# Two transformer layers on one core: denominators of the first element, the projection's order, and a matmul behind its filler

## The chip, the cores and the metric

The kernel runs on one core of one Trainium2 chip. A core has a matmul engine (TensorE, PE in the profile), VectorE (DVE), ScalarE (ACT), GpSimd (POOL) and a queue engine for transfers (SyncE, SP). The metric is the device time of one launch in microseconds, lower being better; a change is named by its ratio to the time before. All data is fp32.

## The reference

Sixteen elements of shape 256 channels x 32 x 32, that is 1024 positions, go through two layers:

```python
# layer 0, 4 heads of 64
qkv = (xs @ w_proj + b_proj).reshape(B, S, 4, 3 * 64)
attn = softmax(einsum('bihd,bjhd->bijh', q, k) * 64 ** -0.5, axis=2)
res = einsum('bijh,bjhd->bihd', attn, v).reshape(B, S, 256)
x = res @ w_out + b_out + xs
...
# layer 1, 8 heads of 32
x = x + attention(group_norm(x, gn1_w, gn1_b), qkv_w, proj_w, proj_b, phys_bias)
h = group_norm(x, gn2_w, gn2_b)
h = gelu(einsum('oc,bchw->bohw', mlp_w1, h) + mlp_b1)
x = x + einsum('oc,bchw->bohw', mlp_w2, h) + mlp_b2
```

A softmax is an exponential divided by its row's sum. The kernel works with unnormalised exponentials, sums them, and multiplies the result of the attention by the inverse of the sum, called the denominator below (`den`). There is no search for a maximum; the sums of all denominators and of their inverses go into two totals (`dsum`, `isum`) that are looked at once at the end, and a second, general pass runs if they were out of range.

## The kernel before

**Stages.** The elements run one after the other, and the work of neighbours overlaps. For each element b: the first attention (`attention_a`, layer 0), projection of its result (`o`), a group norm, the second attention (`attention_b`, layer 1), its projection (`j`), a second group norm, and the MLP in two halves (`hidden`, `outputs`), whose matmuls use a seven-product scheme for 2x2 blocks. The MLP of element b is used as filler for element b+1: its first half fills the time between the two attentions, and its second half, pieces `m`, goes into the steps of the second attention. The input projections of the next element (`qk_a`, `v_a`; a list `first` of 12 pieces for element 0, eight for query and key and four for value) fill what is left. A piece of these is two matmuls of 128x128x512 (query, key) or four of 128x128x256 (value). Element 0 has no MLP before it: between its two attentions stand the 12 pieces of `first`, and the later steps of its second attention have no filler. Elements 1 to 14, "middle elements", are alike; their keys and queries are made by seven products.

**An attention.** The positions are worked in two query halves t of 512, and the heads in two channel groups c: four items. For each item the loop goes over eight blocks of 128 keys. `scores` gives `s` in PSUM, ScalarE the exponential `e`, `weigh` the product with the values (`acc`), and VectorE adds the exponentials into `es`. A step of the second attention takes two key blocks. After an item, TensorE sums `es` over the partitions into `den`.

**Inverting.** `denominators` (L375) has ScalarE copy `den` out of PSUM (L376), a transfer spreads it over all partitions (L381), VectorE inverts the 128x16 that come out (L387), transfers bring the inverse to DRAM and back, spread as wide as the result (L391 or L398, L403), and later `then` multiplies (L510 or L707). It is a chain of steps counted by `later.after(n, fn)`: `fn` runs at the n-th tick from then, and a step of an attention has one tick. In the first attention one `den` serves both items of a query half (`normalise`, L479). In the second attention of middle elements each item's `es` is first folded to half by two transfers into `packed` (`fold`, L651), the second of which adds; three or four ticks later `normalise_folded` (L659) makes `den`.

**Order inside a step.** `run` (L1253) ticks, which issues what is due, and then runs the step's filler pieces; each engine works through its instructions in the order they come in, apart from a scheduler that moves some of them where nothing forbids it.

**The projection.** `out_proj` (L737) makes two output halves co from two input halves kc, with 128x32 column tiles inside an attention (`cols[0]` below 128). There both output halves lie in one PSUM tile, and its loop is output half first: co 0 from kc 0, co 0 from kc 1, co 1 from kc 0, co 1 from kc 1. Input half kc 1 is the item normalised last. In middle elements the result goes by ScalarE into a place in `packed` (`home`, slots 2 and 3) and is added a step later.

**Places.** PSUM has two banks b0 and b1 and three tiles of two banks (`wide`). Scores of the first key block of a step of the second attention use b0 and b1, and a `wide`; `acc` uses b0; `den` of the second attention uses b1. `packed` has four slots: item 0's folded sums in 0 and 1, item 1's in 2 and 3, item 2's again in 0 and 1. Products 6 and 7 of the MLP put their results into slots 2 and 3 (`number - 4`), once `normalise_folded` of item 1 has declared the place as free.

Of the kernel before, what the change touches and what calls it, by code (L numbers as in the profile page):

```python
# [14 lines left out]
P = 128  # L15
# [4 lines left out]
TB = 512  # L20
# [239 lines left out]
def first_pass(ctx, tc, x, out, k):  # L260
# [109 lines left out]
    def weights_tile(name):  # L370
        return work.tile([P, 4, TB], F32, tag="e", name=name, bufs=4)

    spread_out, spare = {}, {}

    def denominators(key, den, d, full, waits, then, parts=1):  # L375
        nc.scalar.copy(d, den)  # L376
# [34 lines left out]

    def attention_a(b, qT, kT, v, project):
        key, D, lag = f"a_{b}", D0, 2
        items = [(t, c) for t in range(NT) for c in range(CC)]
        units = [(i, kb) for i in range(len(items)) for kb in range(SB)]
        res = act.tile([P, CC, S], F32, tag="res", name=f"res_{key}")
        accs, held, sums, both, pair = {}, {}, {}, {}, []

        def scores(i, kb):
            t, c = items[i]
# [18 lines left out]
        def weigh(i, kb, e):  # L441
            t, c = items[i]
            if kb == 0:
                if i % 2:
                    acc = wide(f"acc_{key}_{i}", 2)
                    accs[i] = [acc[:, h, :] for h in range(2)]
                else:
                    accs[i] = [bank(f"acc_{key}_{i}_{h}", h) for h in range(2)]
            for h in range(2):
                for g in range(2):  # L450
                    nc.tensor.matmul(  # L451
                        accs[i][h][g * D : (g + 1) * D, :],
                        v[h * HALF : (h + 1) * HALF, kb, c * 2 + g],
                        e[h * HALF : (h + 1) * HALF, g, :],
                        start=(kb == 0),
                        stop=(kb == SB - 1),
                    )
            if kb == 0:
                held[i] = e
                return  # L460
            if kb == 1:
                if c == 0:
                    both[t] = work.tile([P, 2 * CC, TB], F32, tag="es", name=f"es_{key}_{t}", bufs=2)
                sums[i] = both[t][:, 2 * c : 2 * c + 2]
            spread_out["es"] = nc.vector.tensor_add(  # L465
                sums[i], held[i] if kb == 1 else sums[i], e
            )
            if kb == SB - 1:
                r = res[:, c, t * TB : (t + 1) * TB]
                one, two = accs.pop(i)  # L470
                nc.scalar.copy(r, one)
                nc.vector.tensor_add(r, r, two)  # L472
                if i == len(items) - 1:
                    kept.discard(2)
                if c == CC - 1:
                    later.after(2 if t < NT - 1 else 1, lambda: normalise(t))


        def normalise(t):  # L479
            half = TB // 2  # L480
# [63 lines left out]
    def attention_b(b, qT, kT, v, project):  # L544
# [106 lines left out]
        def fold(i, r):  # L651
            if i == 0:
                packs.append(act.tile([P, 4, TB], F32, tag="res", name=f"packed_{key}"))
            packed = packs[0][:, i % 2 * 2 : i % 2 * 2 + 2]
            nc.sync.dma_start(packed, sums[i][:HALF])
            nc.gpsimd.dma_start(packed, sums[i][HALF:], accum_op=ALU.add)
            later.after(3 if i == 1 else 4, lambda: normalise_folded(i, r, packed))

        def normalise_folded(i, r, packed):  # L659
            c = items[i][1]  # L660
            q = TB // G
            den = bank(f"den_{key}_{i}", 1)[:, :q]
            for m in range(2):
                for n in range(G):
                    nc.tensor.matmul(
                        den[n * D : (n + 1) * D, :], k["folded"][:, c, m],
                        packed[:, m, n * q : (n + 1) * q], start=m == 0, stop=m == 1,
                    )
            if i == 1:
                spare["home"] = packs[0]  # L670
            full = work.tile([P, TB], F32, tag="full", name=f"rd_{key}_{i}", bufs=2)
            denominators(
                f"{key}_{i}", den, full[:, :q], full, (1, 2 if i < 2 else 4),
                lambda full: scale(i, r, False, full), G,
            )

        def normalise(i, r, last):
            t, c = items[i]
            at_end = last and b == B - 1
            den = bank(f"den_{key}_{i}", 1)  # L680
            for g in range(G):
                nc.tensor.matmul(
                    den[g * D : (g + 1) * D, :],
                    k["eones"][:, c * G + g],
                    sums[i][:, g, :],
                    start=True,
                    stop=True,
                )
            full = work.tile([P, TB], F32, tag="full", name=f"rd_{key}_{i}", bufs=2)
            if at_end:  # L690

                nc.vector.reciprocal(full, den)
                scale(i, r, last, full)
                for tot, what in ((dsum, den), (isum, full)):
                    part = small.tile([P, 1], F32, tag="part", name="part")
                    nc.vector.tensor_reduce(part, what, AX.X, ALU.add)
                    nc.gpsimd.tensor_add(tot[:, :1], tot[:, :1], part)
# [39 lines left out]
    def out_proj(key, w, src, bias, xs, t, stats, then):  # L737
        todo = list(range(CC))

        def issue(cos=range(CC), apart=False):  # L740
            home = None if apart else spare.pop("home", None)
            apart = apart or cols[0] == P
            if not apart:
                both = wide(f"{key}_{t}")
            ps = {}

            def leave(co):
                y = xs[:, co, t * TB : (t + 1) * TB]
# [12 lines left out]
                todo.remove(co)  # L761

            def add_up(co, y, held):
                with tc.issue_after(spread_out["es"].ins):
                    nc.vector.tensor_add(y, y, held)
                    nc.vector.bn_stats(stats[:, co, t, :], y)

            for co in cos:
                ps[co] = bank(f"{key}_{t}_{co}", co) if apart else both[:, co, :]
                for kc in range(CC):  # L770
                    product(
                        ps[co],
                        w[:, kc, co * P : (co + 1) * P],
                        src(kc),
                        start=(kc == 0),
                        stop=(kc == CC - 1),
                    )
                if apart:
                    leave(co)
            if not apart:  # L780
                for co in cos:
                    leave(co)
            if not todo and then:
                then()
# [312 lines left out]
    def mlp(b, xb):  # L1097
# [93 lines left out]
        def reduce(number, right, outs, then, part=0, parts=1):  # L1191
# [14 lines left out]
            if len(outs) == 2 or "home" in spare:  # L1206
# [3 lines left out]
                if len(outs) == 2:  # L1210
                    m = lent[0][:, number % 4]
                else:
                    m = spare["home"][:, number - 4]
                if bias is not None:
                    nc.scalar.activation(m[:, at], ps, AF.Identity, bias=bias[:, co : co + 1])
                    bias = None
# [36 lines left out]
    def run(stage, fill=None):  # L1253
        for n, _ in enumerate(stage):
# [3 lines left out]
            later.tick()  # L1258
            if n <= last:
                run_pieces(pieces, False)  # L1260

    def run_pieces(pieces, tick=True):
        for piece in pieces:
# [79 lines left out]
    for b in range(B):  # L1343
        def load_next(b=b):
# [13 lines left out]
            attention_0(  # L1358
                b, tiles0, xs[b],
                lambda st, b=b, xn=xn, seven=seven, sums_1=sums_1: group_norm(  # L1360
                    f"g{b}", xs[b], st, k["g1w"], k["g1b"], "res", xn, 2 if b else 3,
                    (lambda y: sums_1.update(input_sums(f"b{b}", y))) if seven else None,
                ),
            )
# [43 lines left out]
        own = [lambda: early(v[1]), qk[n], v[2], qk[n + 1], v[3], *qk[n + 2 :]]  # L1408
        now, end = outputs, []
        if b == 0:  # L1410
            first = []
        if b == B - 1:

            now, end = outputs[:3], outputs[3:]
        if not first:

            fill = {m: [piece] for m, piece in enumerate(own[:5:2] + own[1::2] + own[6:])}
            fill.update({len(own) + 3 * m: [piece] for m, piece in enumerate(now)})
            now = []

        if first:
            o = [
                [lambda piece=piece, part=part: piece(part, 2) for part in range(2)]
                for piece in now
            ]
# [319 lines left out]
```

## Time and profile before

| | us |
|---|---|
| median of 3 runs | 3612.91 |
| lowest, highest | 3612.54, 3613.1 |
| the profiled execution's own time | 3610.05 |
| span of its instructions | 3608.0 |
| DVE add of exponentials in `attention_b`, 128x2048, 460 of them | 1.935 each |
| ACT exponential in `attention_b`, 1280 of them | 0.865 each |

The profile holds one execution. A line of its timeline has the start in us, the time from the first start to the last end of a group of like instructions, engine, source line, operation, output tile <- inputs, shape and count, and in brackets how long the engine stood idle before it and what ended that. PE is matmuls and PEld weight loads. A fp32 matmul leaves two records. Ends on PE are modelled, starts are measured. Times are counted from the start of the span.

### The profile page before, as it was taken

What the parts mean: (1) busy time and instruction counts of PE and PEld (TensorE: products, weight loads), DVE (VectorE), ACT (ScalarE), POOL (GpSimd) and SP (SyncE); (2) the same over time, 40 slices, a digit from 0 to 9 for tenths busy, and PEclk for the clock granted to TensorE, in tenths of its full rate; (3) what the DMA queues carried; (4) which work ended last, traced back from release to release, by engine and by line L of the source; (5) the groups of instructions that cost most, each with busy time, mean ns of one, the idle gap of its engine ahead of it and who ended that gap; (6) DMA issues with size and microseconds to landing.
All of it is one profiled execution on the core that took longest, in us unless ns stands there. A gap on an engine that the chain in (4) does not pass through costs nothing.

```text
span 3608.0 us, 81721 instructions
## 1 busy us (share of the span) xinstructions
PE 3584.1 (99%) x35573; PEld 1470.7 (41%) x35573; DVE 2780.1 (77%) x3181; ACT 2282.7 (63%) x3196; POOL 232.0 (6%) x317
## 2 busy tenths in 40 slices
PE   9999999999999999999999999999999999999999
PEld 4434344343443434434344443434434444343433
DVE  5686887868777687876878878688786977868787
ACT  4665757657575675756658566585765757657572
POOL 3000100001000010000000001000010100000000
PEclk9999999999999999999999999999999999999999
DMA  3010311213122131211312113121121212213100
GB/s 130 10 60 30 73 63 37 75 34 86 45 43 69 39 81 45 48 64 39 81 45 52 66 33 81 45 55 63 38 76 45 55 63 47 73 39 64 51 28 28
DMA packets 81572, 198.30 MB, mean 55 GB/s; under 512 B 37974, under 2 KB 38742, under 8 KB 75062
## 3 DMA queue, kind: packets, MB, share of 16 engines
q1 hardware_dynamic: 71828, 164.39, 14.6%
q0 software_dynamic: 7632, 28.21, 5.1%
q8 instruction: 281, 4.60, 0.5%
q14 instruction: 85, 0.70, 0.1%
q10 hardware_dynamic: 1746, 0.40, 0.1%
HBM read 125.85 MB, written 22.27 MB: 41 GB/s over the span
## 4 chain that ended last, share of the span: by engine, by line
PE 80%; DVE 10%; issue 5%; DMA 3%; SPq 2%; ACT 1%; DVEq 0%; POOL 0%
PE s_a L428 12%; PE acc_a L451 12%; PE m L1109 10%; PE s_b L571 8%; PE acc_b L625 7%; PE m L357 6%; DVE es_b L599 5%; PE qk_b L1015 3%; PE qk_a L1015 3%; PE v_b L357 3%; PE o L357 3%; PE j L357 3%; PE v_a L357 2%; DMA rd_b<-row_b 2%; PE qk7y_b L1015 1%
## 5 line engine op out<-in xcount | busy, mean ns | idle before, releaser
L584 ACT ACTIVATE e_b<-s_b 128x1024 f32<-128x1024 f32 (+1 forms) x1280 | 982.0, 865 | 136.9 <-PE s_b L571 136.3
L599 DVE TENSOR_TENSOR es_b<-es_b,e_b 128x2048 f32<-128x2048 f32 (+1 forms) x460 | 881.8, 1935 | 102.3 <-ACT e_b L584 85.9
L438 ACT ACTIVATE e_a<-s_a 128x1024 f32<-128x1024 f32 x512 | 520.7, 1024 | 361.0 <-PE s_a L428 359.0
L428 PE MATMUL s_a<-q,k 64*64 64x512 f32 x4096 | 544.2, 593 | 0.7 <-DVE res_a L472 0.7
L451 PE MATMUL acc_a<-e_a,v 64*64 64x512 f32 x4096 | 540.1, 589 | 0.0
L571 PE MATMUL s_b<-q,k 32*64 32x512 f32 x8192 | 527.3, 600 | 4.0 <-DVE res_b L643 2.0
L465 DVE TENSOR_TENSOR es_a<-es_a,e_a 128x1024 f32<-128x1024 f32 x384 | 470.4, 1225 | 70.7 <-ACT e_a L438 51.7
L625 PE MATMUL acc_b<-e_b,v 128*32 128x512 f32 x4096 | 492.1, 598 | 0.0
L357 PE MATMUL m<-g,w 128*32 128x256 f32 (+2 forms) x6464 | 416.6, 385 | 0.0
L357 PEld LDWEIGHTS m<-g,w 128*32 128x32 f32 (+1 forms) x6464 | 224.2, 111 | 203.8 <-issue 57.7
L451 PEld LDWEIGHTS acc_a<-e_a,v 64*64 64x64 f32 x4096 | 187.9, 133 | 251.5 <-issue 215.2
L571 PEld LDWEIGHTS s_b<-q,k 32*64 32x64 f32 x8192 | 175.7, 130 | 257.5 <-issue 132.7
L428 PEld LDWEIGHTS s_a<-q,k 64*64 64x64 f32 x4096 | 175.9, 133 | 247.5 <-issue 209.2
L625 PEld LDWEIGHTS acc_b<-e_b,v 128*32 128x32 f32 x4096 | 108.5, 109 | 351.5 <-ACT e_b L584 194.7
L1109 PE MATMUL m<-gn_h,w 128*128 128x512 f32 x512 | 242.2, 601 | 2.3 <-DVE x L1230 1.3
L599 DVE TENSOR_TENSOR es_b<-e_b,e_b 128x2048 f32<-128x2048 f32 (+1 forms) x72 | 147.0, 2052 | 124.5 <-ACT e_b L584 124.5
L1173 DVE TENSOR_TENSOR g<-g,g 128x512 f32<-128x512 f32 (+1 forms) x185 | 196.0, 1070 | 1.2 <-PE m L357 0.8
L1109 PE MATMUL m<-hs,w 128*128 128x512 f32 x384 | 178.1, 592 | 0.1
L1124 ACT ACTIVATE g<-g,m1b 128x512 f32<-128x512 f32 x128 | 92.1, 720 | 108.8 <-DVE g L1153 81.3
L1109 PEld LDWEIGHTS m<-gn_h,w 128*128 128x128 f32 x512 | 93.2, 190 | 117.7 <-issue 100.2
L1124 ACT ACTIVATE g<-m,m1b 128x512 f32<-128x512 f32 x128 | 80.9, 683 | 77.9 <-PE m L1109 77.9
L357 PE MATMUL v_a<-wp,x 128*32 128x256 f32 (+1 forms) x1856 | 121.5, 379 | 0.0
(217 smaller groups left out, 3537.8 us busy)
## 6 DMA issues: line engine op xcount, KB each, us to landing
w<-w_kept SPq DMA_DIRECT2D x30, 1792.0 KB
packed_b<-es_b SPq DMA_DIRECT2D x42, 512.0 KB
packed_b<-es_b POOLq DMA_DIRECT2D x42, 512.0 KB, 6.2
d_a<-row_a SPq DMA_DIRECT2D x64, 256.0 KB
rd_b<-row_b SPq DMA_DIRECT2D x252, 64.0 KB
out_dram<-x SPq DMA_DIRECT2D x63, 256.0 KB
x<-in_x_dram SPq DMA_DIRECT2D x30, 512.0 KB
qk<-qk_kept SPq DMA_DIRECT2D x14, 1024.0 KB
```

Of the source, the lines that this page charges most:

```text
L357: nc.tensor.matmul(o[sl], w[:, sl], r, **flags)
L428: nc.tensor.matmul(s[h : h + HALF, g, :], kT[g * D : (g + 1) * D, c, kb * P + h : kb * P + h + HALF], qT[g * D : (g + 1) * D, c, t * TB : ...
L438: nc.scalar.activation(e, s, AF.Exp, scale=float(D) ** -0.5)
L451: nc.tensor.matmul(accs[i][h][g * D : (g + 1) * D, :], v[h * HALF : (h + 1) * HALF, kb, c * 2 + g], e[h * HALF : (h + 1) * HALF, g, :], st ...
L465: spread_out["es"] = nc.vector.tensor_add(sums[i], held[i] if kb == 1 else sums[i], e)
L571: nc.tensor.matmul(outs[g][h : h + HALF, :], kT[g * D : (g + 1) * D, c, k0 : k0 + HALF], qT[g * D : (g + 1) * D, c, t * TB : (t + 1) * TB] ...
L584: spread_out["exp"] = nc.scalar.activation(to, s, AF.Exp, scale=float(D) ** -0.5)
L599: ins = nc.vector.tensor_add(d, (d if kb else es[0][:, g : g + step]), es[m][:, g : g + step])
L625: nc.tensor.matmul(acc[g * D : (g + 1) * D, :], v[:, kb + m, c * G + g], es[m][:, g, :], start=(m == 0), stop=(m == 1),)
L1015: nc.tensor.matmul(to, w, x[right], start=first, stop=True, skip_group_check=not first)
L1109: nc.tensor.matmul(ps, blocks[1][number - 1][:, i * P : (i + 1) * P], inputs[b][number], start=first, stop=True, skip_group_check=not first,)
L1173: (nc.vector.tensor_add if plus else nc.vector.tensor_sub)(d, d, more)
```

## The change

Element 0: in its first attention the second query half no longer takes the way through DMA. `normalise_item` makes a `den` for each of its two items. For the third item (first of the half) ScalarE copies `den` into SBUF and VectorE inverts the copy; for the fourth VectorE inverts from PSUM; then VectorE multiplies, and later reduces both for the totals (`add_to_range`, which also replaces the same lines in the last element). Five pieces of `first` stay between the attentions, and seven go into steps 8 to 14 of the second attention. The first group norm waits one tick in place of three.

All elements with a projection inside the attention: the loop is input half first, so both output halves from kc 0, then both from kc 1.

Middle elements: `normalise_folded` of item 1 is put on a list `trailing`, which `run` empties after the step's filler pieces. `packed` is declared as free for the filler when item 1 is folded, and product 6 writes slot 0 in place of 2.

```diff
@@ attention_a
+        def normalise_item(i):
+            t, c = items[i]
+            den = wide(f"den_{key}_{i}", next(m for m in order if m != 2))[:, 0, :]
+            for j in range(4):
+                nc.tensor.matmul(
+                    den[j * 32 : (j + 1) * 32, :], k["ones"], sums[i][:, j // 2, :],
+                    start=True, stop=True,
+                )
+            if not c:
+                homes.append(act.tile([P, CC, S], F32, tag="k1", name=f"d_{key}_{t}"))
+            full, held_den = homes[0][:, c, :TB], homes[0][:, c, TB:]
+            r = res[:, c, t * TB : (t + 1) * TB]
+            if c < CC - 1:
+                nc.scalar.copy(held_den, den)
+                den = held_den
+            tc.keep_in_program_order(nc.vector.reciprocal(full, den))
+            tc.keep_in_program_order(nc.vector.tensor_mul(r, r, full))
+            if c == CC - 1:
+                later.after(2, lambda: project(t, res)())
+            later.after(3, lambda: add_to_range(den, full))
...
-                if c == CC - 1:
+                if t == NT - 1 and not b:
+                    if c < CC - 1:
+                        later.after(2, lambda: normalise_item(i))
+                    else:
+                        normalise_item(i)
+                elif c == CC - 1:
                     later.after(2 if t < NT - 1 else 1, lambda: normalise(t))
@@ add_to_range
+    def add_to_range(den, inverse):
+        for tot, what in ((dsum, den), (isum, inverse)):
+            part = small.tile([P, 1], F32, tag="part", name="part")
+            nc.vector.tensor_reduce(part, what, AX.X, ALU.add)
+            nc.gpsimd.tensor_add(tot[:, :1], tot[:, :1], part)
@@ fold
-            later.after(3 if i == 1 else 4, lambda: normalise_folded(i, r, packed))
+            if i == 1:
+                spare["home"] = packs[0]
+                later.after(3, lambda: trailing.append(lambda: normalise_folded(i, r, packed)))
+            else:
+                later.after(4, lambda: normalise_folded(i, r, packed))
@@ out_proj
+            if apart:
+                for co in cos:
+                    for kc in range(CC):
+                        part(co, kc)
+                    leave(co)
+            else:
                 for kc in range(CC):
...
+                    for co in cos:
+                        part(co, kc)
                 for co in cos:
                     leave(co)
@@ reduce
-                    m = spare["home"][:, number - 4]
+                    m = spare["home"][:, number % 6 * 3]
@@ run
             if n <= last:
                 run_pieces(pieces, False)
+            while trailing:
+                trailing.pop(0)()
@@ the loop over elements
-                    f"g{b}", xs[b], st, k["g1w"], k["g1b"], "res", xn, 2 if b else 3,
+                    f"g{b}", xs[b], st, k["g1w"], k["g1b"], "res", xn, 2 if b else 1,
...
-            run_pieces(first if b == 0 else hidden)
+            run_pieces(first[:5] if b == 0 else hidden)
...
-            first = []
+            now, first = first[5:], []
...
-            fill.update({len(own) + 3 * m: [piece] for m, piece in enumerate(now)})
+            at = (len(own), 3) if b else (len(own) + 1, 1)
+            fill.update({at[0] + at[1] * m: [piece] for m, piece in enumerate(now)})
```

More of the change, by code (lines that the diff above doesn't have):

```diff
@@ L371, in weights_tile @@
         return work.tile([P, 4, TB], F32, tag="e", name=name, bufs=4)
-    spread_out, spare = {}, {}
+    spread_out, spare, trailing = {}, {}, []
     def denominators(key, den, d, full, waits, then, parts=1):
@@ L418, in attention_a @@
         res = act.tile([P, CC, S], F32, tag="res", name=f"res_{key}")
-        accs, held, sums, both, pair = {}, {}, {}, {}, []
+        accs, held, sums, both, pair, homes = {}, {}, {}, {}, [], []
         def scores(i, kb):
@@ L668, in normalise_folded @@
                     )
-            if i == 1:
-                spare["home"] = packs[0]
             full = work.tile([P, TB], F32, tag="full", name=f"rd_{key}_{i}", bufs=2)
@@ L693, in normalise @@
                 scale(i, r, last, full)
[L694 to L697, printed above, removed]
+                add_to_range(den, full)
                 return
@@ L766, in add_up, with part @@
                     nc.vector.bn_stats(stats[:, co, t, :], y)
+            def part(co, kc):
+                product(
+                    ps[co],
+                    w[:, kc, co * P : (co + 1) * P],
+                    src(kc),
+                    start=(kc == 0),
+                    stop=(kc == CC - 1),
+                )
             for co in cos:
                 ps[co] = bank(f"{key}_{t}_{co}", co) if apart else both[:, co, :]
-                for kc in range(CC):
[L771 to L780, printed above, removed]
+            if apart:
[4 more added lines that the diff above has]
+            else:
+                for kc in range(CC):
+                    for co in cos:
+                        part(co, kc)
                 for co in cos:
@@ L1410, in first_pass @@
         if b == 0:
-            first = []
+            now, first = first[5:], []
         if b == B - 1:
             now, end = outputs[:3], outputs[3:]
+        o = [
+            [lambda piece=piece, part=part: piece(part, 2) for part in range(2)]
+            for piece in outputs
+        ]
         if not first:
             fill = {m: [piece] for m, piece in enumerate(own[:5:2] + own[1::2] + own[6:])}
-            fill.update({len(own) + 3 * m: [piece] for m, piece in enumerate(now)})
+            at = (len(own), 3) if b else (len(own) + 1, 1)
+            fill.update({at[0] + at[1] * m: [piece] for m, piece in enumerate(now)})
             now = []
         if first:
[L1422 to L1425, printed above, removed]
             fill = dict(enumerate((
```

## The prediction, made before the changed kernel had run

> **What bounds the kernel now.** First the page: one core, clock 1.0 in every slice, and
>
> ```profile
> PE 3584.1 (99%) x35573; PEld 1470.7 (41%) x35573; DVE 2780.1 (77%) x3181; ACT 2282.7 (63%) x3196; POOL 232.0 (6%) x317
> ```
>
> PE's ends are modelled, so 99% hides small waits. I read them from the starts: a group of matmul records that stands undisturbed repeats to a few ns (8 records of `s_a` or `acc_a` 0.858 us, 32 of `s_b` 1.905, 16 of `acc_b` 1.74), and what a group takes beyond that is a wait. Summed over the span this is 66 us: everything else is TensorE at its rate, so only what removes TensorE work or such a wait can pay. Then the list of waits on PE, which names the largest:
>
> ```profile
> PE j L357 <- DVE res_b L707: 9.8, 14, 1.6
> PE s_b L571 <- DVE res_b L643: 2.0, 3, 0.9
> ```
>
> Fourteen times is once in each middle element. The timeline of one of them (element 1):
>
> ```profile
> 420.73 1.04 PE L357 MATMUL j<-res_b,wpj 128*32 128x512 f32 x8
> ...
> 423.06 2.78 PE L357 MATMUL j<-res_b,wpj 128*32 128x512 f32 x24 [1.30 <-DVE res_b L707]
> ...
> 425.78 2.54 PE L571 MATMUL s_b<-q,k 32*64 32x512 f32 x32
> ```
>
> The projection issues 8 of its 32 records, then stands until VectorE has scaled the second half of the result. It takes 425.78-420.73 = 5.05 us; in element 0, where nothing waits, 206.62 to 210.05 = 3.43. The same two starts in all 14 middle elements give 0.58 to 1.93 us too much, 14.3 in sum (0.15 of each is restarting after the wait).
>
> Element 0, second attention, later steps:
>
> ```profile
> 170.64 1.04 PE L682 MATMUL den_b<-es_b,eones 128*32 128x512 f32 x8
> ...
> 171.64 2.81 PE L571 MATMUL s_b<-q,k 32*64 32x512 f32 x32
> ...
> 171.80 0.63 ACT L376 COPY rd_b<-den_b 128x512 f32<-128x512 f32 x1
> ...
> 174.38 1.92 PE L625 MATMUL acc_b<-e_b,v 128*32 128x512 f32 x16
> ...
> 176.24 1.07 PE L571 MATMUL s_b<-q,k 32*64 32x512 f32 x2
> ```
>
> A step without filler lasts 176.24-171.64 = 4.60 us though its matmuls need 3.65: VectorE (41.88 of 45.92 us busy from 165.85 to 211.77) and the copies hold it. Note the second thing: scores that directly follow a `den` stand 2.74-1.90 = 0.84 us, until ScalarE has emptied bank b1, which both use (copy ends 172.43, the weight load resumes 172.49).
>
> **The Trainium skill.** "PSUM — Partial Sum Buffer", Terms, has two engines on one bank and quadrant at once as an error; so scores into b1 must wait out the copy of `den`. The trace agrees (0.84 us above). "VectorE: DVE Perf Modes", First, the fixed hardware budget, calls Reciprocal an iterative divide; the trace agrees: 3366 ns for 128x512 (L692) against 692 for a copy of that shape (L891). "TensorEngine Tiling (Array Packing)", Key Properties, has tiles working in parallel; the trace: a projection piece as four 128x32 column tiles takes 1.83 us, whole 1.716, so moving pieces into the attention costs 0.11 each.
>
> **Part 1, element 0, end of the first attention.** Before, PE ran without a gap from 85.12 (last `acc_a` out) to 114.18 (first `qk_b`), 29.06 us; 12 projection pieces covered the inversion of the denominators (through DMA) and the normalisation. Seven pieces leave: 7 x 1.716 = -12.0. Items 2 and 3 get a `den` each, in place of one shared: 8 records x 0.107 = +0.86. The DMA round (three kinds of issue on SP) goes; VectorE gets it: after the add of item 3's third block, that is from 77.5, it must do a reciprocal (3.37), one add (1.22), the multiply (0.69) and two reductions (0.64, 0.69 as in L696) before the last four adds, which run at 1.14 us from start to start. 77.45 + 3.3 + 1.15 + 0.6 + 1.25 = 83.7; + 3 x 1.14 + 1.22 = 88.4. The new `den` of item 3 needs all of these adds and now stands in PE's order AHEAD of the projection of the first query half; PE is free for it at 85.12 + 0.86 = 85.98. Wait: +2.4 to 2.6, take 2.5. Behind it PE has 3.4 us of projection and one piece (1.7), and VectorE meanwhile inverts from PSUM (89.5 to 92.9), adds one output, multiplies (to 94.2): just before the second projection at 94.5, so nothing. The normalisation's chain (statistics of the last output at about 100.1, means, variances, GpSimd's power, first two scalings) then stands against pieces in which 5.1 us of PE are left; from the trace's gaps (variances' matmul 110.50 to second scaling 113.4) it just fits: 0 to 0.7, take 0.1. Sum -12.0 + 0.86 + 2.5 + 0.1 = -8.5 (bounds -6.5 and -9.3). The wait shortened from 3 steps to 1 is in this order already.
>
> **Part 2, element 0, second attention.** Seven pieces stand at steps 8 to 14, in column tiles: 7 x 1.835 = +12.85. What takes them in are the waits of the steps from 171.64 on, read as above: 0.84, 1.25, 0.88, 1.98, 0.84, 1.25, 0.88 = 7.9, and about 0.5 of restarts between `acc_b` and `s_b`. The 1.15 at 165.85 is ahead of the first piece and stays. As control: steps with own filler earlier in this attention take 5.48 (133.84 to 139.33), which is their matmuls alone, so ScalarE's extra 0.6 us copy fits. +4.2 to +4.9, take +4.5. Element 0: -4.0.
>
> **Part 3, projection by input half, 14 elements.** Both output halves' matmuls of input half 0 now stand ahead of the first that needs the late half: 16 records in place of 8, 0.86 us more cover. ScalarE's emptying started after the whole projection before (425.91), so nothing is lost there; the 0.57 us that the next scores wait for it stays.
>
> **Part 4, den behind filler, 14 elements.** Item 1's `den` (16 records, 0.44 us) moves behind product 6 (64 records, 3.57 us); product 6's ScalarE copies go ahead of `den`'s, and its result to a free slot. PE's work is the same, but `den` now stands directly ahead of scores that use b1. Before, it was
>
> ```profile
> 394.89 0.62 PE L665 MATMUL den_b<-packed_b,folded 128*32 128x128 f32 x16
> ...
> 395.33 3.64 PE L357 MATMUL m<-g,w 128*32 128x256 f32 x64
> ...
> 396.51 0.34 ACT L376 COPY rd_b<-den_b 128x128 f32<-128x128 f32 x1
> ...
> 398.89 1.97 PE L571 MATMUL s_b<-q,k 32*64 32x512 f32 x32
> ```
>
> and the filler hid the copy. Without that cover: 0.14 to 0.17 from `den`'s last record to the copy (as at 171.80), 0.34 copy, 0.05 to resume = 0.53 us, 14 x = +7.4. Does it shift the late half too? No: VectorE is behind there, idle 0.21 us in all from before `den` until the reciprocal 14.7 us after it, which starts at the end of a queue of adds; so the scaling stays where it is while PE reaches the projection 0.53 later. `den`'s own chain has room: spread out, it landed at 402.35, lands near 403.3, and is read at 409.60. Per element the wait (without restart) is then max(0, w-0.86-0.53), with w from 0.43 to 1.78: two elements keep 0.08 and 0.39. So the projection gives 14.3-0.8 = -13.5, and the middle elements -13.5 + 7.4 = -6.1. If the shift did not help, 11.3 in place of 13.5: -3.9.
>
> **Sum.** -4.0 - 6.1 = -10.1 us. The profiled execution took 3610.05 (span 3608.0), so 3599.95; the median of the runs lies 2.86 above it (3612.91), so 3602.8.
>
> **Rivals.** (A) The scores do not wait for `den`'s copy, because something I don't see keeps ScalarE ahead: -4.0 - 13.5 = -17.5, 3595.4. For it: the wait is nowhere in the trace of before at this place. Against: the same pair of instructions shows 0.84 in element 0. (B) Part 1's waits are larger (VectorE's lag also delays ScalarE's exponentials, the normalisation isn't covered by five pieces): element 0 at about +1, and with the unhelped projection -3.9: -3, 3610. For it: five pieces for a chain of 15 us leave margins of some tenths. Against: exponentials have four buffers, of which the lag fills two. (C) Slower: `den`'s copy comes late on ScalarE. Before, it started 1.62 us after `den`'s first record, 1.0 after its results were there. If ScalarE is that busy in the new place too and more, at 2.0 us of wait, the cost is 28 against 14.3 + 4.0: about +9.7, 3622.6. It decides from 25.5/14 = 1.82 us per element. Against: that ScalarE was held by exponentials that end at 396.20, and the new place is 2.7 us later, behind one 0.47 us copy. (D) That the change doesn't do what it says: in the new order of instructions the projection's wait for VectorE stands after half of its matmuls, where the old has it after a quarter, so this is left out.
>
> **How the numbers follow.** Forecast 58%, A 10%, B 22%, C 10%. 0.2%, which is about what a measurement of this kernel tells from no change, is 7.2 us: below 3605.7 is faster. Forecast and A are faster (68%), B the same (22%), C slower (10%). The forecast's own range is 3599.5 to 3606 (part 1 and 2 by 1.5, the shift by 2.2); with A's and B's near sides 3596.5 to 3609.5.
>
> **What would show it.** Right: no wait of `j` on the late half, or under 0.4 us, in 12 of 14 elements; `s_b` after item 1's `den` 2.4 us in place of 1.9; in element 0 a wait of 2 to 3 us ahead of item 3's `den`, first `qk_b` near 105.7, steps of 5.5 us up to the end of its second attention. Wrong: the scores' wait well off 0.53, the projection still standing, or `qk_b` of element 0 later than 109.

## The result, and the profile after

The changed kernel takes 3604.3 us (median of 11 runs, 3602.69 to 3606.52) and the kernel before, on the same chip, 3613.43 us (11 runs, 3610.7 to 3615.41): ratio 0.9975, 95% interval 0.9966 to 0.9984, or 9.1 us less. The profiled executions differ by 6.2 us (spans 3608.0 and 3601.8). TensorE is as full as before, as the page's first part has it:

```profile
PE 3584.2 (100%) x35705; PEld 1470.2 (41%) x35705; DVE 2786.2 (77%) x3187; ACT 2283.0 (63%) x3196; POOL 219.1 (6%) x319
```

The list of TensorE's waits in the changed kernel (engine, tile and line waiting, what it waited for, us in total, times, longest) shows what became of the largest:

```profile
PE den_a L493 <- DVE es_a L471: 2.6, 1, 2.6
PE o L357 <- DVE res_a L541: 1.5, 2, 0.8
```

The projection `j`, 9.8 us in 14 waits before, is gone from the top (0.4 us in two waits are left in this list), and a single new wait of 2.6 us leads. The timeline of element 1 answers to the projection shown before (start, duration, engine, line, operation, tiles, shape, records):

```profile
418.54 3.67 PE L357 MATMUL j<-res_b,wpj 128*32 128x512 f32 x32
422.15 1.11 PE L602 MATMUL s_b<-q,k 32*64 32x512 f32 x16
```

All 32 records now stand in one group, and 422.15 - 418.54 = 3.61 us replaces 5.05. The price is at item 1's denominators, in the same element (TensorE, then ScalarE):

```profile
392.26 3.63 PE L357 MATMUL m<-g,w 128*32 128x256 f32 x64
395.71 0.62 PE L700 MATMUL den_b<-packed_b,folded 128*32 128x128 f32 x16
396.26 2.42 PE L602 MATMUL s_b<-q,k 32*64 32x512 f32 x32
398.61 1.92 PE L656 MATMUL acc_b<-e_b,v 128*32 128x512 f32 x16
```

```profile
396.40 0.27 ACT L376 COPY rd_b<-den_b 128x128 f32<-128x128 f32 x1
```

The scores behind `den` take 398.61 - 396.26 = 2.35 us where an undisturbed group takes 1.90, because ScalarE copies bank b1 out from 396.40 to 396.67. This is so in all 14 elements.

Element 0, end of the first attention: TensorE before, TensorE after, then VectorE after.

```profile
82.44 2.75 PE L451 MATMUL acc_a<-e_a,v 64*64 64x512 f32 x24
...
114.18 2.31 PE L357 MATMUL qk_b<-gn_g,wq 128*128 128x512 f32 x5
```

```profile
83.72 2.75 PE L457 MATMUL acc_a<-e_a,v 64*64 64x512 f32 x24
89.05 1.06 PE L493 MATMUL den_a<-es_a,ones 128*32 128x512 f32 x8 [2.58 <-DVE es_a L471]
89.90 3.64 PE L357 MATMUL o<-res_a,wo 128*32 128x512 f32 x32
...
106.18 7.03 PE L357 MATMUL qk_b<-gn_g,wq 128*128 128x512 f32 x16
```

```profile
82.51 1.27 DVE L417 TENSOR_REDUCE part<-d_a 128x1 f32<-128x512 f32 x2
83.69 5.20 DVE L471 TENSOR_TENSOR es_a<-es_a,e_a 128x1024 f32<-128x1024 f32 x4
...
90.17 3.36 DVE L504 RECIPROCAL d_a<-den_a 128x512 f32<-128x512 f32 x1 [0.67 <-PE den_a L493]
```

TensorE stands 2.58 us until VectorE, behind item 2's reductions, has done its last four adds. The first `qk_b` moved from 114.18 to 106.18. In the second attention that follows, the steps that had waits now hold a piece each and run at their matmuls' rate:

```profile
170.88 1.98 PE L602 MATMUL s_b<-q,k 32*64 32x512 f32 x32
172.79 1.92 PE L656 MATMUL acc_b<-e_b,v 128*32 128x512 f32 x16
174.53 1.90 PE L357 MATMUL qk_a<-x,wp 128*32 128x512 f32 x16
176.36 1.97 PE L602 MATMUL s_b<-q,k 32*64 32x512 f32 x32
```

One step is 176.36 - 170.88 = 5.48 us, the sum of its undisturbed groups (1.905 + 1.74 + 1.835).

For the middle elements I add up, over all 14, the time from the start of one group of matmuls to the start of the next, so that the last column but one is the whole second attention. A wait counted so includes the restart behind it, and is longer than in the list of waits:

| kernel | projection `j` | `den`'s wait for folded sums | scores behind `den`, beyond 1.90 | second attention | against before |
|---|---|---|---|---|---|
| before | 62.30 | 0.0 | 0.0 | 1449.52 | |
| changed | 51.17 | 0.0 | 6.2 | 1444.71 | -4.8 |
| only the first element's change (E1) | 60.93 | 3.0 | 0.0 | 1451.33 | +1.8 |
| only the projection (E2) | 53.86 | 1.6 | 0.0 | 1442.85 | -6.7 |
| only `den` behind (E3) | 60.93 | 0.0 | 6.2 | 1454.38 | +4.9 |
| changed, `den` ahead (E4) | 51.33 | 2.9 | 0.0 | 1441.58 | -7.9 |
| changed, `den` between (E5) | 52.79 | 0.0 | 0.0 | 1440.10 | -9.4 |
| changed, other buffer (E6) | 53.22 | 0.0 | 0.0 | 1440.51 | -9.0 |
| E6, reductions late (E7) | 53.43 | 0.0 | 0.0 | 1440.66 | -8.9 |
| E7, reciprocal early (E10) | 49.65 | 0.0 | 0.0 | 1436.87 | -12.7 |
| changed, pieces stay (E8) | 51.72 | 0.0 | 6.2 | 1445.18 | -4.3 |
| changed, round by DMA (E9) | 51.50 | 0.0 | 6.2 | 1445.05 | -4.5 |

Each row is one execution. How much such a row varies is seen where the middle elements run the same program: the changed kernel, E8 and E9 lie within 0.5 us of each other in the last column, E6 and E7 within 0.2, but before and E1 1.8 apart.

### The profile page after: what moved, and what is told of

Same layout as the page of the kernel before. It is cut to its first block, busy times and chain, and to the rows that moved or that the text cites. A ratio compares the mean times of both kernels' runs of the same rounds, so it can differ in the third digit from the quotient of the medians.

```text
span 3601.8 us, 81991 instructions
## 1 busy us (share of the span) xinstructions
PE 3584.2 (100%) x35705; PEld 1470.2 (41%) x35705; DVE 2786.2 (77%) x3187; ACT 2283.0 (63%) x3196; POOL 219.1 (6%) x319
## 4 chain that ended last, share of the span: by engine, by line
PE 92%; DVE 4%; issue 2%; DMA 1%; SPq 1%; ACT 1%; DVEq 0%; POOL 0%
PE s_b L602 12%; PE s_a L434 12%; PE acc_a L457 12%; PE acc_b L656 11%; PE m L357 10%; PE m L1146 10%; PE qk_b L1052 4%; PE qk_a L1052 3%; PE v_b L357 3%; PE j L357 3%; PE v_a L357 3%; PE o L357 3%; PE qk7y_b L1052 1%; PE qk7y_a L1052 1%; DVE es_b L630 1%
## 5 line engine op out<-in xcount | busy, mean ns | idle before, releaser
L630 DVE TENSOR_TENSOR es_b<-es_b,e_b 128x2048 f32<-128x2048 f32 (+1 forms) x460 | 881.5, 1934 | 104.7 <-ACT e_b L615 88.3
```

The costliest lines, as they stand in the source:

```text
L630: ins = nc.vector.tensor_add(d, (d if kb else es[0][:, g : g + step]), es[m][:, g : g + step])
```

## The experiments

All times are medians beside the kernel before on the same chip (3613.52 for E1 to E4, 3614.0 for E5 to E7, 3612.94 for E8 and E9, 3613.16 for E10). Diffs are against the changed kernel unless said.

**One part at a time: E1 to E3.** E1 has only the first element's change. It puts back two orders, that of the projection and that of `den`:

```diff
-            if i == 1:
-                spare["home"] = packs[0]
-                later.after(3, lambda: trailing.append(lambda: normalise_folded(i, r, packed)))
-            else:
-                later.after(4, lambda: normalise_folded(i, r, packed))
+            later.after(3 if i == 1 else 4, lambda: normalise_folded(i, r, packed))
...
+            if i == 1:
+                spare["home"] = packs[0]
...
-                for kc in range(CC):
-                    for co in cos:
+                for co in cos:
+                    for kc in range(CC):
                         part(co, kc)
...
-                    m = spare["home"][:, number % 6 * 3]
+                    m = spare["home"][:, number - 4]
```

> Only the changes to element 0; the projection's order and the place of den are those of before. My theory: -4 us, all of it before element 1's first scores (start at about 208.9 in place of 213.1); the middle elements as before, with j waiting in each. Rival (the gain of element 0 is lost again because the next elements wait for transfers that now come sooner relative to their use): 0 us, with the lead gone within element 1.

Measured: 3608.75, ratio 0.9986 (0.998 to 0.9993), -4.8 us. Element 0 does what it does in the changed kernel (second attention from 115.17, element 1 from 209.22, 3.9 earlier than before), so its gain needs neither of the other parts. Its waits show something I had not looked for:

```profile
PE j L357 <- DVE res_b L735: 8.5, 12, 1.3
PE den_a L493 <- DVE es_a L471: 2.6, 1, 2.6
PE den_b L696 <- DMA packed_b<-es_b: 2.1, 4, 0.8
```

With `den` ahead of its filler it waits in some elements (6 of 14, by the starts) for the transfer that folds the sums. No such wait stands in the profiled execution of the kernel before, which has the same order.

E2 has the projection's order alone (`den` is put back as in E1):

```diff
-                if t == NT - 1 and not b:
+                if False:
...
-                    f"g{b}", xs[b], st, k["g1w"], k["g1b"], "res", xn, 2 if b else 1,
+                    f"g{b}", xs[b], st, k["g1w"], k["g1b"], "res", xn, 2 if b else 3,
...
-            run_pieces(first[:5] if b == 0 else hidden)
+            run_pieces(first if b == 0 else hidden)
...
-            now, first = first[5:], []
+            first = []
...
-            at = (len(own), 3) if b else (len(own) + 1, 1)
+            at = (len(own), 3)
```

> Only the projection by input half. My theory: the wait of j shrinks by 0.86 us in each middle element, -11 us in sum (from the waits of the profile of before), and nothing else moves; j takes 3.5 us in most elements. Rival (the wait moves on: VectorE, whose scaling comes no sooner, is met again at the next scores or at the last den): -4 us or less, with s_b or den of the same element waiting longer by what j waits less.

Measured: 3603.66, ratio 0.9973 (0.9963 to 0.9984), -9.9 us. The projection falls by 62.30 - 53.86 = 8.4 in the profiled execution, less than the 11 expected. This part alone brings what the whole change brings.

E3 has `den` behind its filler alone (the edits of E1 for the projection and of E2).

> Only den of item 1 behind its filler. My theory: the scores behind it wait 0.45 to 0.55 us, but the projection's wait shrinks by the same, as its late half doesn't move: 0 us (-1 to +2). Rival 1 (the two waits add): +7 us, j's waits as before. Rival 2 (den behind filler pays by itself, since den waited for its folded sums): faster by 3 us or more.

Measured: 3614.77, ratio 1.0004 (0.9996 to 1.0012), +1.3 us, which the interval does not tell from no change. The scores wait 6.2 us in sum, and the projection, reached 0.45 later in each element, gives back only 1.4 (60.93 against 62.30), not as much as the scores wait: in this execution VectorE scales the late half 89.63 us after the stage's start, the mean of 14, against 89.29 in the profile of before. Against the profiled execution of before that is +4.9; the medians show less. The folded sums' waits, which this order removes (0.0 in it, 1.6 to 3.0 in E1, E2 and E4), are of the missing size. That the usual execution of the kernel before has them I infer from its medians, 2.9 to 4.0 us above its profiled execution, and from E1, which has its middle elements, has 3.0 us of these waits, and was profiled in an execution that took just its median; it is not shown.

**Is `den` behind its filler worth it? E4, E5, E6.** E4 is the changed kernel with item 1's `den` ahead of product 6 again:

```diff
-            if i == 1:
-                spare["home"] = packs[0]
-                later.after(3, lambda: trailing.append(lambda: normalise_folded(i, r, packed)))
-            else:
-                later.after(4, lambda: normalise_folded(i, r, packed))
+            later.after(3 if i == 1 else 4, lambda: normalise_folded(i, r, packed))
...
-                    m = spare["home"][:, number % 6 * 3]
+                    m = spare["home"][:, number - 4]
```

> The changed kernel with den of item 1 ahead of its filler again. My theory: the scores' wait of 0.45 us and den's own 0.11 go, 14 x = 7.7 us, of which the projection, reached sooner, gives back 2: -15 us against before, 5 to 6 us faster than the changed kernel. Rival (den ahead of filler waits for the folded sums' transfer once PE is ahead): as the changed kernel, -9, with matmuls ahead of den (acc_b) taking over 1.74 us.

Measured: 3599.31, ratio 0.996 (0.9947 to 0.9974), -14.2 us, 5 below the changed kernel by the differences to before. It is close to the sum of the other two parts alone (E1 and E2: -4.77 - 9.86 = -14.63). So `den` behind its filler isn't worth it as it stands. But the rival is true in part:

```profile
PE den_b L696 <- DMA packed_b<-es_b: 2.1, 3, 0.8
```

Both places cost: behind it the copy, ahead of it the transfer. If that is all, a place with filler on both sides costs nothing. E5 puts `den` between product 6's two halves:

```diff
             if n <= last:
-                run_pieces(pieces, False)
+                for piece in pieces:
+                    run_pieces([piece], False)
+                    while trailing:
+                        trailing.pop(0)()
```

> The changed kernel with item 1's denominators between the two halves of product 6 in the middle elements (the result still goes to the changed kernel's slot): 1.74 us of filler ahead of them, 1.74 behind. My theory: behind the filler they cost only because the next scores wait for ScalarE's copy of bank b1, and ahead of it they cost only because they wait for the transfers of the folded sums (0.8 us in 3 of 14 elements). Between the halves both are covered: scores behind item 1's denominators back at 1.90 us in all 14 elements (2.35 in the changed kernel), no wait of these denominators on packed_b, 6 to 7 us below the changed kernel, -16 against the kernel before. Rival, that the position itself costs (VectorE's queue later, whatever the bank does): half of the 5.0 us between the two kernels tried before, -12.

Measured: 3599.57, ratio 0.996 (0.9947 to 0.9974), -14.4 us. On TensorE it is as my theory has it, in all 14 elements:

```profile
392.03 1.91 PE L357 MATMUL m<-g,w 128*32 128x256 f32 x32
393.76 0.62 PE L700 MATMUL den_b<-packed_b,folded 128*32 128x128 f32 x16
394.19 1.91 PE L357 MATMUL m<-g,w 128*32 128x256 f32 x32
396.03 1.97 PE L602 MATMUL s_b<-q,k 32*64 32x512 f32 x32
397.94 1.92 PE L656 MATMUL acc_b<-e_b,v 128*32 128x512 f32 x16
```

The scores take 397.94 - 396.03 = 1.91, and `den` waits for nothing. The time misses the -16 expected by 1.6, and 1.6 us came back in the projection (52.79 against 51.17 in the changed kernel), which TensorE now reaches 0.45 earlier while the late half does not come earlier. Against E4 the profiled executions show 1.5 us less in the middle elements (-9.4 for -7.9); the medians do not show it.

E6 keeps the changed kernel's order and gives `den` another buffer:

```diff
-            den = bank(f"den_{key}_{i}", 1)[:, :q]
+            if i == 1:
+                den = wide(f"den_{key}_{i}")[:, 0, :q]
+            else:
+                den = bank(f"den_{key}_{i}", 1)[:, :q]
```

> The changed kernel, order kept (item 1's denominators behind product 6, directly ahead of the scores), but these denominators are written to one of the wide score buffers, the one that the following scores use last (their records 25 to 32, 1.4 us later), not to bank b1. My theory: the wait belongs to the bank, so it goes: scores behind them 1.90 to 1.95 us in place of 2.35, 14 x 0.44 = 6.2 us below the changed kernel, -15.5 against the kernel before. Rival, that the scores wait for something else there (matmuls restarting after small ones, ScalarE's exponentials later): 2.35 stays and the time is the changed kernel's, -9 against the kernel before.

Measured: 3597.87, ratio 0.9954 (0.9941 to 0.9968), -16.1 us, 7 below the changed kernel. With the order unchanged, the wait goes with the bank:

```profile
397.04 0.62 PE L703 MATMUL den_b<-packed_b,folded 128*32 128x128 f32 x16
397.58 1.97 PE L602 MATMUL s_b<-q,k 32*64 32x512 f32 x32
399.49 1.07 PE L656 MATMUL acc_b<-e_b,v 128*32 128x512 f32 x8
```

399.49 - 397.58 = 1.91 against 2.35. This shows the mechanism of part 4: the wait belongs to the bank. E4, E5 and E6 can't be told apart by their times; their intervals overlap.

**The new wait in element 0: E7** is E6 with item 2's reductions put off until the group norm has scaled its input:

```diff
             if c == CC - 1:
                 later.after(2, lambda: project(t, res)())
-            later.after(3, lambda: add_to_range(den, full))
+                later.after(3, lambda: add_to_range(den, full))
+            else:
+
+                def reduce_late():
+                    with tc.issue_after(spare["scaled"].ins):
+                        add_to_range(den, full)
+
+                spare["reduce"] = reduce_late
...
-                    nc.vector.tensor_scalar(
+                    spare["scaled"] = nc.vector.tensor_scalar(
...
         later.flush()
+        if b == 0:
+            spare["reduce"]()
```

> As the kernel with the other buffer, and in element 0 the two reductions of item 2's denominators (0.64 us each on VectorE) put off until the normalised input is scaled; before, they stood between the normalisation of item 2 and the last four adds of the sums. My theory: the wait ahead of item 3's denominators is VectorE's queue, so it falls from 2.6 to 1.3 us, the first qk_b starts at 104.9 in place of 106.2 and the time is 1.3 us below the kernel with the other buffer alone (-17 against the kernel before). Rival, that the adds wait for exponentials or that the chain of the normalisation takes over: the wait falls by less than 0.5 us or qk_b does not start earlier.

Measured: 3596.75, ratio 0.9952 (0.9938 to 0.9965), -17.2 us.

```profile
87.95 1.06 PE L493 MATMUL den_a<-es_a,ones 128*32 128x512 f32 x8 [1.39 <-DVE es_a L471]
...
105.09 7.03 PE L357 MATMUL qk_b<-gn_g,wq 128*128 128x512 f32 x16
```

The wait fell from 2.58 to 1.39 and `qk_b` starts 1.09 earlier than in the changed kernel (106.18): the part that went was VectorE's queue. The times of E6 and E7 can't be told apart.

**Which part of element 0's change pays? E8, E9.** E8 leaves all twelve pieces where they were and keeps the inversion by VectorE:

```diff
-            run_pieces(first[:5] if b == 0 else hidden)
+            run_pieces(first if b == 0 else hidden)
...
-            now, first = first[5:], []
+            now, first = [], []
```

> The changed kernel with all twelve pieces of the next element's first projection left at the end of element 0's first attention (none at steps 8 to 14 of its second attention); items 2 and 3 still get their own denominators, inverted by VectorE. By the prediction's steps: the 7 x 1.716 = 12.0 us come back, so the second attention starts at 114.87 + 12.0 = 126.9; the second attention loses the pieces and has its waits again, 90.25 us as in the kernel before in place of 94.05; element 1 starts at 217.1, 8.2 later than in the changed kernel, and the time is 8.2 us above the changed kernel's (about -1 against the kernel before). So the inversion on VectorE by itself costs about 4 us, and the gain is the pieces'. Rival, that VectorE's inversion is itself the gain: second attention from 122.9 or earlier.

Measured: 3612.68, ratio 0.9999 (0.999 to 1.0008), -0.3 us. The second attention starts at 128.87, 14.0 later than in the changed kernel; about 1.7 of that is a stretch of half clock (last section), and the rest, 12.3, is the pieces (12.0 expected). It lasts 219.16 - 128.87 = 90.29, as before. Element 1 starts at 219.16, 6.0 later than in the kernel before (213.11) and 4.3 later without the half clock, so the inversion on VectorE by itself costs about what was expected (4). The medians tell no change from the kernel before.

E9 moves the seven pieces but keeps the round by DMA:

```diff
-                if t == NT - 1 and not b:
+                if False:
```

> The changed kernel with items 2 and 3 of element 0 normalised as before (one set of denominators for both, spread out by DMA, inverted as 128x16 and brought back), but the seven pieces moved all the same: five pieces have to cover the round. From the trace of the kernel before: first output half done at 89.55, five pieces to 98.13, result scaled at 98.6 (wait 0.5), second half of the projection to 102.1, its statistics to 103.8, then the chain of the normalisation, 4.1 us from its first small matmul, with no filler left: first qk_b at about 108.4, 2.2 later than in the changed kernel, time 2.2 us above it (-7 against the kernel before). Rival, that DMA's landing is later with less between, or that the uncovered chain is longer: 110 or later. Rival, that the inversion by VectorE gives nothing: 106.2.

Measured: 3608.42, ratio 0.9987 (0.9979 to 0.9996), -4.5 us. Five pieces almost cover the round, but nothing is left to cover the chain of the normalisation:

```profile
104.78 0.38 PE L357 MATMUL gm_g<-mean_c_g,gavg 128*128 128x2 f32 x2 [2.02 <-DVE mean_c_g L853]
106.00 0.38 PE L357 MATMUL gv_g<-dv_g,gavg 128*128 128x2 f32 x2 [0.84 <-DVE dv_g L865]
...
108.60 10.20 PE L357 MATMUL qk_b<-gn_g,wq 128*128 128x512 f32 x16 [2.22 <-DVE gn_g L885]
118.63 1.89 PE L357 MATMUL v_b<-wq,gn_g 128*128 128x256 f32 x8
```

`qk_b` starts at 108.60 (estimated 108.4). That it then takes 118.63 - 108.60 = 10.0 us in place of 6.9 I had not expected; it is the clock again. So the seven pieces are the gain, and VectorE's inversion makes it 2.4 us larger by leaving pieces for the chain, plus what half clock costs.

**The rest of the projection's wait: E10.** In every kernel but this one item 1's reciprocal stands 77.2 us after its stage's start (77.5 in four elements of all), whatever TensorE does, and the scaling comes 11.5 to 13.5 us later, when the inverse has landed. E10 is E7 with the reciprocal issued together with `den`:

```diff
-        later.after(waits[0], invert)
+        if waits[0]:
+            later.after(waits[0], invert)
+        else:
+            invert()
...
-                f"{key}_{i}", den, full[:, :q], full, (1, 2 if i < 2 else 4),
+                f"{key}_{i}", den, full[:, :q], full, (0, 3) if i == 1 else (1, 2 if i < 2 else 4),
```

> The kernel with the other buffer and the late reductions, and item 1's reciprocal in the middle elements issued with its denominators, so that it stands on VectorE ahead of the two adds that follow (4.67 us) and not behind them; its scaling stays in its step. My theory: what is left of the projection's wait for the late half (5.4 us over 14 elements against 3.43, of which 1.7 is the step to the following scores) is VectorE waiting for the inverted denominators' transfer (idle 1.9 to 3.3 us ahead of the scaling, released by rd_b<-row_b). With the reciprocal 5.2 us earlier the transfer has landed: that idle time goes, every middle element's projection takes 3.55 us, 3.7 us less in sum, -20 against the kernel before. Rival: the transfers on SP's queue, now ahead of the folded sums of item 2, make these late, and item 2's denominators wait: time unchanged or above.

Measured: 3592.4, ratio 0.9941 (0.9927 to 0.9955), -20.8 us, the best of all. VectorE in E7 and then in E10:

```profile
405.23 0.25 DVE L387 RECIPROCAL inv_b<-sp_b 128x16 f32<-128x16 f32 x1
...
417.33 0.69 DVE L747 TENSOR_TENSOR res_b<-res_b,rd_b 128x512 f32<-128x512 f32 x1 [2.27 <-DMA rd_b<-row_b]
```

```profile
399.71 0.24 DVE L387 RECIPROCAL inv_b<-sp_b 128x16 f32<-128x16 f32 x1
...
414.66 0.69 DVE L750 TENSOR_TENSOR res_b<-res_b,rd_b 128x512 f32<-128x512 f32 x1
```

The wait for the transfer is gone, and every middle element's projection takes 3.55 us. Its slowest run (3592.83) lies below the fastest of E7 (3595.68), and no `den` waits for its folded sums, which the rival expected.

## Why the prediction was right, and which terms were off

The forecast was -10.1 us and 3602.8; measured -9.1 and 3604.3. All four parts have the sign and the place given to them, and the signs named in advance came: `j` waits over 0.4 us in one element of 14, the scores behind `den` take 2.35 for 2.4, `qk_b` starts at 106.18 for 105.7, the steps take 5.48. Rival A (no cost of `den`) is refuted by the 2.35 us in all 14 elements. Rival B's size is refuted by element 0, which gained 4.2; of its mechanisms the uncovered normalisation shows in E9 alone. In rival C the copy had to be late; it starts 0.69 us after `den`'s first record, every time.

- **Part 1**, -8.5: measured -8.0 (`qk_b` at 106.18 for 105.7). The wait ahead of item 3's `den` is 2.58 for 2.5. The term that was small is the second `den`: the last `acc_a` group starts 1.28 later than before (83.72 for 82.44), 0.14 of which the first attention already started later; so 1.14 for item 2's `den`, where 0.86 was put.
- **Part 2**, +4.5: measured +3.8 (second attention 94.05 for 90.25 us). The seven steps' waits took in 9.0 of the 12.85 where 8.4 was read. Element 0 is -4.2 for -4.0.
- **Part 3**, -13.5: measured 62.30 - 51.17 = -11.1. Two things went wrong with this term. The 14.3 was counted from 3.43, a group that `acc_b` follows; where scores follow, a group that waits for nothing takes 3.55 (E10: all 14 elements). So 14 x 0.12 = 1.7 of the 14.3 was no wait; the prediction had it in the 0.15 called restart, which was to go with the wait. And 51.17 - 49.65 = 1.5 stayed as waits, in 5 elements where 2 were expected. The prediction took the late half's time from one execution, but it is a transfer's landing, 11.5 to 13.5 us after the reciprocal.
- **Part 4**, +7.4: measured +6.2, since the copy took 0.27 us there, not 0.34. The step that the late half is not shifted with `den` holds nearly: the reciprocal stands at 77.2 us in all kernels of its order, and the scaling starts, in the mean of 14, 89.3 to 89.5 us after the stage's start where `j` starts at 88.3 to 88.5, and 89.4 to 89.6 in the four kernels where it starts at 88.75 (changed, E3, E8, E9). So `j` starting 0.45 later waits less: 51.17 to 51.72 in the changed kernel, E8 and E9, against 52.79 to 53.43 in E5, E6 and E7, 1.7 in the mean where the prediction had 2.2. Why the scores must wait, no run separates: the prediction names a rule on two engines in one bank, but they also overwrite the place that the copy still reads.
- **Part 4, what was put at nothing:** ahead of its filler `den` can wait for the folded sums. Its profile before showed none of it, and the prediction looked for no wait that the move takes away. It is worth 1.6 to 3.0 us in three kernels (E1, E2, E4), less than the copy.
- **The sum.** The middle elements gave -4.8 for -6.1, with element 0 -9.0. The profiled executions differ by only 6.2 since this one of the changed kernel has 2.8 more elsewhere, part of it waits for landings in the first attention (`o` on `res_a`, 1.5 us). The prediction carried the 2.86 us between one execution and the median over unchanged; it is itself made of waits that vary. That the sum of the terms and the medians agree to 0.1 is therefore partly luck. So is the sum itself: the parts are off by +0.5, -0.7, +2.4 and -1.2, the projection's smaller gain against the smaller cost of `den`, and leave 1.0.

## What to carry to other kernels

Where a matmul writes a bank that the next group also writes, look for filler behind it that covers the copy out of the bank, and for filler ahead of it if its own inputs may be late; if there is one filler, split it or take another bank, which came to the same here. When more cover on the waiting engine is a gain, look next at what the late input waits for: here one small reciprocal behind two long adds in a queue set the start of a transfer, and moving it took away what the cover had left. Waits for transfers, read from one execution, are a sample: look for the same wait in kernels of the same order before pricing it at nothing.

## What the runs showed of the hardware that was not expected

After some stands TensorE ran at half clock. The activity by windows, for the changed kernel and then for E6 (window, sum, busy us and records of PE, PEld, DVE, ACT, POOL, granted clock, DMA share, GB/s), shows the same work at the same time:

```profile
86.40:89.05 2.65, 0.07 (x5) 0.04 (x2) 2.55 (x3) 0.58 (x1) 0.00 (x0) 1.00 0.00 0
...
89.90:93.00 3.10, 3.10 (x36) 1.10 (x28) 2.83 (x1) 0.00 (x0) 0.00 (x0) 1.00 0.00 0
```

```profile
86.40:89.05 2.65, 0.07 (x5) 0.04 (x2) 2.55 (x3) 0.58 (x1) 0.00 (x0) 1.00 0.00 0
...
89.90:93.00 3.10, 3.10 (x20) 1.08 (x16) 2.75 (x1) 0.00 (x0) 0.00 (x0) 0.50 0.00 0
```

After the same stand of 2.58 us the granted clock was 1.00 in one and 0.50 in the other, with 36 matmul records in 3.10 us against 20. It was 0.50 for 3.41 us in E4, E6 and E8 and cost about 1.7 us; the changed kernel, E1 and E5, with the same stand, had none of it, nor had E7 with 1.39 us. In E9, whose stands were 2.02, 0.84 and 2.22 us close together, it lasted 6.83 us and cost some 3.2. The Trainium skill, "TensorE: Matmul & The Clock Gate", Part 1, has a free-running window of 3413 ns by whose activity the clock is set. The traces agree: the clock's changes lie at multiples of 3.41 us from its first rise, which comes 4.4 to 5.8 us into the span (in E6 the rise is at 4.55 and the loss at 89.88, 25 x 3.413 later). The three kernels with a first rise at 4.38 to 4.73 us had the stand inside one window, but for 0.07 us in E4, and lost the clock; those with 5.26 to 5.84 had it cut in two (in the changed kernel 0.70 and 1.88 us). So a stand of 2.6 us cost 2.6 or 4.3 us, by chance, and a shorter one was worth more than its length. It also bears on medians: 1.7 us of an execution may be this. The mean clock of every run hints at how often: it reads 0.999 in place of 1.000 in 23 of the 59 runs of the six kernels with the stand of 2.58 us, in all 12 of E9, in none of the 10 of E7 and E10, and in 3 of 77 of the kernel before. Within the six kernels the runs at 0.999 are 1.2 us longer in the mean, unevenly (2.7 in E6, -0.3 in E4).
